# Sliding-window attention between two FFNs: turning the probabilities with VectorE's 32x32 transposes and copies inside SBUF instead of on TensorE

## The chip, the cores and the metric

The kernel runs on one core of one Trainium2 chip. The metric is the device time of one execution in microseconds (us), the median of several runs. The engines are PE (TensorE, matrix products), DVE (VectorE), ACT (ScalarE), POOL (GpSimd) and SP (SyncE, which only issues DMAs here). Everything is computed in fp32.

## The reference

Four sequences of 256 tokens, 512 wide, go through an FFN, an attention and the same FFN again, each on the layer-normalized input and added to it (the FFNs by half). The FFN is a 512x512 linear layer plus a mixture of 8 low-rank experts (rank 16, the best 2 of 8 by a router). The attention has 32 query heads, 8 key-value heads, a head dimension of 128, rotary embedding, and a causal window of 128 keys:

```python
q = _rope((x @ wq).reshape(B, S, 32, 128), pos)
k = _rope((x @ wk).reshape(B, S, 8, 128), pos)
v = (x @ wv).reshape(B, S, 8, 128)
scores = einsum('bqhgd,bshd->bhgqs', q.reshape(B, S, 8, 4, 128), k) * 128 ** -0.5
allowed = (j <= i) & (j > i - 128)
attn = softmax(where(allowed, scores, finfo.min))
out = einsum('bhgqs,bshd->bqhgd', attn, v).reshape(B, S, 4096) @ wo
```

## The kernel before, in words

The 1024 tokens are cut in two halves of two sequences. The first FFN runs over both halves, then the attention, then the second FFN. The attention is made of 32 **units** (h, g, b): half h, group g (a key-value head with its four query heads), sequence b of the half (lists at L842 and L843, main loop L960 to L1076). While a unit's softmax runs on the other engines, TensorE computes projections for later groups and output products of the unit before. All the projections use seven half-size products in place of eight, so sums of weights, of tokens and of results are formed on DVE and POOL.

A unit has 256 queries x 4 heads. They are taken in 8 blocks of 32 queries (4 with the first 128 tokens, 4 with the second), so that a block's 4 heads x 32 queries fill the 128 partitions. The steps of one unit:

- `scores` (L684): four products `sa` with the first 128 keys; DVE adds the mask and takes the row's maximum in one operation (L696) that writes into `probs`. Four products `sb` for the second 128 queries, each with the 128 keys of its window and a few more; DVE puts the right keys in place (L714) and takes maxima (L716).
- `exponentials` (L720): two small DVE operations make the negated, scaled maxima `nm` (L722, L723), then ACT takes 8 exponentials into `probs` with the row sums as a by-product.
- `normalize` (L734): a reciprocal on DVE and two multiplications of 128x512 on POOL (L738), in place on `probs`.
- `transposes` (L742): TensorE turns the 8 blocks (L746), so that keys lie on the partitions; ACT copies the first four out of PSUM (L750). Of the second four, the key rows belong partly to the first and partly to the second 128 tokens: DVE multiplies them by the 0/1 tiles `old` and `new` (L755) into two tiles.
- `values` (L761): `oa`, one product of 128x512 with the values for the first 128 queries, and `ob`, two of them for the second (L768); ACT copies both to `oT` (L771). `outputs` (L777) multiplies `oT` with the output weights (`y`, L794), in four steps that are put on the queue `late` and run inside the next unit.

The order of the instructions on PE, DVE, POOL and ACT is the order of the code (`manual_schedule`, L874 to L880; PE's and DVE's until three units are left). There is one buffer `probs`, so the next unit's `scores` follow this unit's `transposes` in the order. What runs around them depends on the unit:

- b = 0: the next group's `queries` (L517, steps "1" to "7"), mixed with the rest by a string (L979), in which "n" is `normalize`, "t" `transposes`, "y" an output product and "a", "w", "v", "k", "c", "d", "e" are FFN steps and sums: `"1yn6a27cy5d4yte3yw"`. Step "7" ends with DVE's `v` add (L512), "5" begins with the next add. The query results are rotated on DVE with the tables `cos_sb` and `sin_sb` (L484, L486) and summed on POOL (L492).
- b = 1: the next group's `keys` (L580, on odd n) or `project_values` (L624, on even n), in parts `both`, `second`, `others` (L995 to L1021), followed by sums of weights, a load of wk or wv on SP and output products.
- the last three units have no projections left; second-FFN steps fill them.

`transposes` are called by the string for b = 0 and otherwise at L1040 and L1041, just before the next unit's `scores`. The order of the loads on SP is found by a scheduler.

Of the kernel before, what the change touches and what calls it, by code (L numbers as in the profile page):

```python
# [29 lines left out]
BLK = 32  # L30
NB = P // BLK
EPS = 1e-5
SCALING = 32.0 / 16.0
SM_SCALE = HD ** -0.5
# [4 lines left out]
def macaron_kernel(  # L39
# [45 lines left out]
    cos_sb = const.tile([HD, S], F32, name="cos_sb")  # L85
    nc.sync.dma_start(out=cos_sb, in_=cos[:, :S])
    sin_sb = const.tile([HD, S], F32, name="sin_sb")
    nc.sync.dma_start(out=sin_sb, in_=sin[:, :S])

    weights = {}  # L90

# [118 lines left out]
        return bass.AP(tensor=w.tensor, offset=w.offset, ap=[w.ap[0], [-BLK, 2], w.ap[2]])  # L210


    probs = const.tile([P, 2 * NB, P], F32, name="probs")
    for e in range(NB - 1):
        nc.gpsimd.memset(probs[:, e, (e + 1) * BLK :], 0.0)


    old = const.tile([P, NB, BLK], F32, name="old")
# [462 lines left out]
        nc.scalar.copy(vS[h, g][:, i, :], pv[:, : 2 * HD])  # L681


    def scores(h, g, b):  # L684
        o = b * S
        q, k = qT[h, g][:, b], kT[h, g]
        pr = probs
        mx = sb.tile([P, 2 * NB], F32, tag="mx", bufs=3, name=f"mx_{h}_{g}_{b}")
        sm = sb.tile([P, 2 * NB], F32, tag="sm", bufs=3, name=f"sm_{h}_{g}_{b}")
        pa = score_bank(f"sa_{h}_{g}_{b}").rearrange("p (c k) -> p c k", k=P)  # L690
        for e in range(NB):
            n = (e + 1) * BLK
            nc.tensor.matmul(pa[:, e, :n], q[:, e], k[:, o : o + n], start=True, stop=True)  # L693
        for e in range(NB):
            n = (e + 1) * BLK
            nc.vector.tensor_tensor_reduce(  # L696
                pr[:, e, :n], pa[:, e, :n], mask[:, P - n :], SM_SCALE, -3.4e38,
                ALU.add, ALU.max, mx[:, e : e + 1],
            )
        pairs = []  # L700
        for p in range(NB // 2):
            pb = score_bank(f"sb_{h}_{g}_{b}_{p}")
            for r in range(2):

                m = 2 * p + r
                at = r * P + m * BLK
                nc.tensor.matmul(  # L707
                    pb[:, at : at + P + BLK], q[:, NB + m],
                    k[:, o + m * BLK : o + m * BLK + P + BLK], start=True, stop=True,
                )  # L710
# [5 lines left out]
            nc.vector.tensor_reduce(mx[:, NB + 2 * p : NB + 2 * p + 2], pb, AX.X, ALU.max)  # L716
            pairs.append(pb)
        return pr, mx, sm, pairs, f"{h}_{g}_{b}"

    def exponentials(pr, mx, sm, pairs, name):  # L720
        nm = sb.tile([P, 2 * NB], F32, tag="nm", bufs=3, name=f"nm_{name}")
        nc.vector.tensor_scalar(nm[:, :NB], mx[:, :NB], -1.0, None, ALU.mult)  # L722
        nc.vector.tensor_scalar(nm[:, NB:], mx[:, NB:], -SM_SCALE, None, ALU.mult)  # L723
        for n in range(2 * NB):
            keys_of = min(n + 1, NB) * BLK
            src, scale = (
                (pr[:, n, :], 1.0) if n < NB else (pairs[(n - NB) // 2][:, n % 2, :], SM_SCALE)
            )
            nc.scalar.activation(  # L729
                pr[:, n, :keys_of], src[:, :keys_of], AF.Exp, bias=nm[:, n : n + 1], scale=scale,  # L730
                accum_out=sm[:, n : n + 1],
            )

    def normalize(pr, sm):  # L734
        nc.vector.reciprocal(sm, sm)  # L735
        for n in range(0, 2 * NB, NB):
            w = pr[:, n : n + NB, :]
            nc.gpsimd.tensor_tensor(  # L738
                w, w, sm[:, n : n + NB].unsqueeze(2).to_broadcast([P, NB, P]), ALU.mult
            )  # L740

    def transposes(h, g, b, pr):  # L742
        def turn(n0, name):
            pt = ps.tile([P, NB, G, BLK], F32, tag="s", bufs=4, name=f"{name}_{h}_{g}_{b}")
            for e in range(NB):
                nc.tensor.transpose(pt[:, e, :, :], pr[:, n0 + e, :], ident)  # L746
            return pt

        p0 = sb.tile([P, NB, G, BLK], F32, tag="p0", bufs=1, name=f"p0_{h}_{g}_{b}")
        nc.scalar.copy(p0, turn(0, "t0"))  # L750
        pt = turn(NB, "t1")
        parts = []
        for n, w in enumerate((old, new)):
            part = sb.tile([P, NB, G, BLK], F32, tag=f"p1{n}", bufs=1, name=f"p1{n}_{h}_{g}_{b}")
            nc.vector.tensor_tensor(  # L755
                part, pt, w.unsqueeze(2).to_broadcast([P, NB, G, BLK]), ALU.mult
            )
            parts.append(part)
        return p0, parts

    def values(h, g, b, p0, p1):  # L761
        oT = sb.tile([HD, G, S], F32, tag="oT", bufs=4, name=f"oT_{h}_{g}_{b}")
        v = vS[h, g - g % 2]
        cols = ts(g % 2, HD)
        for i, parts in enumerate(([p0], p1)):
            po = mm_bank(f"o{'ab'[i]}_{h}_{g}_{b}")
            for n, part in enumerate(parts):
                nc.tensor.matmul(  # L768
                    po, v[:, 2 * b + n, cols], part, start=(n == 0), stop=(n == len(parts) - 1)
                )  # L770
            nc.scalar.copy(  # L771
                oT[:, :, ts(i, P)].rearrange("p j (e q) -> p e j q", e=NB),
                po.rearrange("p (e j q) -> p e j q", e=NB, j=G),
            )
        return oT

    def outputs(h, g, b, oT):  # L777
# [162 lines left out]
    def run(queue, n):  # L940
        for _ in range(min(n, len(queue))):
            queue.popleft()()
# [17 lines left out]
    for u, (h, g, b) in enumerate(units):  # L960
# [8 lines left out]
            nc.scalar.activation(root, eps, AF.Sqrt)  # L969
        parts = []  # L970

        def turn(at=(h, g, b), pr=ahead[0]):
            parts.extend(transposes(*at, pr))

        if b == 0 and n < len(groups):

            order = {0: "1n6kv2754t3", 4: "1yn6a27cy5d4yte3yw"}[len(late)]  # L979
            steps = queries(*groups[n], nc.vector.tensor_copy, ends)  # L980
            steps |= {
                "y": lambda: run(late, 1), "n": lambda: normalize(ahead[0], ahead[2]),
                "w": lambda: sum_o_weights(h, g), "v": lambda: project_v(0, 0, 2),
                "k": lambda: sum_weights("k", *groups[2]), "a": lambda: fill(left, 1),
                "t": turn, "c": None, "d": None, "e": None,
            }

            if g == NKV - 2 and h + 1 < NHALF:
                more_tokens = sum_tokens(h + 1, *(nc.gpsimd, nc.vector) * 2)
                steps |= {"c": more_tokens[3], "d": more_tokens[1], "e": more_tokens[2]}  # L990
            for step in order:
                if steps[step]:
                    steps[step]()
            ends.pop()()
        elif b == 1 and n + 1 < len(groups):  # L995
            both, second, others = begun
            both()
            run(late, 1)
            if g == NKV - 2 and h + 1 < NHALF:
                more_tokens[4]()  # L1000
            second()
            normalize(ahead[0], ahead[2])
            if n == 2:
                for t in behind:
                    measure(t, "a")
            if n % 2 == 1 and (h, g) != groups[NKV]:
                sum_weights("v", *groups[n + 1])
            others()
            fill(left, 4)
            turned = [behind.popleft() for _ in range(2 if behind and n in (4, 6) else 0)]  # L1010
            for t in turned:
# [8 lines left out]
            for t in turned:  # L1020
# [116 lines left out]
```

## Time and profile before

| | |
|---|---|
| runs, us | 766.15, 765.78, 765.36; median 765.78 |
| span of the profiled execution, us | 764.3 |
| PE busy, us | 757.1 (99%) |
| DVE, POOL, ACT busy, us | 560.1, 541.6, 210.3 (73%, 71%, 28%) |
| moved by DMA | 48.97 MB, mean 64 GB/s |
| transposes on PE (L746), one unit, on the chain | 0.87 us |
| ACT copy of turned blocks (L750) | 32 of 586 ns |
| value products (L768), one unit, on the chain | 0.86 us (oa), 1.72 us (ob) |

The span is the time from the first to the last instruction in the one execution that was profiled; the runs are timed from outside and take some 1.5 us more. A line of the groups or of a timeline names the engine, the line of the code, the operation and the tiles (output<-input), with partitions x elements; in a timeline the first two columns are start and duration in us, and a bracket at the end tells how long the engine had been idle and what released it. The chain is followed back from the last instruction, at each step to whatever it waited for.

### The profile page before, as it was taken

Reading aid. Unit: us, or ns where it says so; the run is one execution under the profiler, and the core shown is the slowest. Engines: PE = TensorE matmul, PEld = TensorE weight load, DVE = VectorE, ACT = ScalarE, POOL = GpSimd, SP = SyncE. Lnnn points to the kernel's source line nnn. Section 1 sums busy time; section 2 is a strip of 40 time slices with the busy share of each in tenths; the row PEclk is TensorE's granted clock in tenths of the full one; section 3 lists DMA queues with packets and bytes.
Section 4 is the critical chain, followed back from the end, with each engine's and each line's share of the span. In section 5 each row is a group of like instructions: output and inputs, shape, how many; then the busy total and the mean of one; then the engine's idle time right before and its main releaser. Section 6 shows DMA issues by size and latency. Waiting matters only on the chain.

```text
span 764.3 us, 11179 instructions
## 1 busy us (share of the span) xinstructions
PE 757.1 (99%) x3894; PEld 633.6 (83%) x3894; DVE 560.1 (73%) x1344; ACT 210.3 (28%) x749; POOL 541.6 (71%) x591
## 2 busy tenths in 40 slices
PE   8999999999999999999999999999999999999998
PEld 6877888888888888888888888888888888888866
DVE  5797885858675867668667867486867867595977
ACT  5421132422223130322222233213042222223331
POOL 6877775848767595769585788759575959865843
PEclk9999999999999999999999999999999999999999
DMA  9302111304030303112030303030301111010001
GB/s 318 123 1 83 52 59 30 109 1 138 1 111 28 111 28 97 42 57 83 20 118 1 129 9 111 28 111 29 107 31 56 56 49 63 1 56 28 2 27 56
DMA packets 29480, 48.97 MB, mean 64 GB/s; under 512 B 1136, under 2 KB 10352, under 8 KB 29424
## 3 DMA queue, kind: packets, MB, share of 16 engines
q1 hardware_dynamic: 29424, 48.26, 18.7%
q8 instruction: 31, 0.51, 0.3%
q14 instruction: 25, 0.20, 0.1%
HBM read 46.15 MB, written 2.10 MB: 63 GB/s over the span
## 4 chain that ended last, share of the span: by engine, by line
PE 96%; DVE 1%; DMA 1%; POOL 0%; SPq 0%; issue 0%; ACT 0%; DVEq 0%; ACTq 0%
PE q L533 25%; PE y L794 25%; PE ob L768 7%; PE k L590 6%; PE v L642 6%; PE sb L707 5%; PE sa L693 4%; PE oa L768 4%; PE t L746 4%; PE p_f L380 3%; PE po_f L380 2%; PE pa_f L344 2%; PE po_f L443 1%; DMA wb_sb<-in_w_base_dram 1%; PE po_f L360 1%; PE y L836 1%
## 5 line engine op out<-in xcount | busy, mean ns | idle before, releaser
L492 POOL TENSOR_TENSOR qT<-ra_q,rb_q 128x512 f32<-128x512 f32 x64 | 81.3, 1272 | 108.6 <-DVE rb_q L486 108.6
L486 DVE TENSOR_TENSOR rb_q<-q,sin_sb 64x512 f32<-64x512 f32 x128 | 88.0, 688 | 1.7
L750 ACT COPY p<-t 128x512 f32<-128x512 f32 x32 | 18.7, 586 | 211.7 <-PE t L746 211.7
L738 POOL TENSOR_TENSOR probs<-probs,sm 128x512 f32<-128x512 f32 x64 | 65.2, 1039 | 15.4 <-DVE sm L735 14.9
L794 PE MATMUL y<-wos,oT 128*128 128x256 f32 x248 | 63.7, 379 | 0.0
L794 PE MATMUL y<-wo,oT 128*128 128x256 f32 x248 | 63.7, 379 | 0.0
L794 PE MATMUL y<-wo,oTs 128*128 128x256 f32 x244 | 62.6, 379 | 0.0
L533 PE MATMUL q<-xs,wq 128*128 128x256 f32 x256 | 60.6, 379 | 0.2 <-DVE rb_k L486 0.2
L533 PE MATMUL q<-xa,wq 128*128 128x256 f32 x256 | 60.6, 379 | 0.0
L533 PE MATMUL q<-xs,wqs 128*128 128x256 f32 x256 | 60.5, 379 | 0.0
L768 PE MATMUL ob<-p,v 128*128 128x512 f32 x128 | 60.2, 592 | 0.0
L484 DVE TENSOR_TENSOR ra_q<-q,cos_sb 128x512 f32<-128x512 f32 x64 | 44.3, 691 | 20.4 <-PE q L533 14.8
L533 PEld LDWEIGHTS q<-xa,wq 128*128 128x128 f32 x256 | 48.4, 190 | 12.4 <-issue 6.2
L771 ACT COPY oT<-oa 128x512 f32<-128x512 f32 x32 | 18.7, 585 | 135.8 <-PE oa L768 135.8
L533 PEld LDWEIGHTS q<-xs,wq 128*128 128x128 f32 x256 | 48.6, 190 | 7.1 <-issue 0.5
L533 PEld LDWEIGHTS q<-xs,wqs 128*128 128x128 f32 x256 | 48.7, 190 | 6.6
L794 PEld LDWEIGHTS y<-wo,oT 128*128 128x128 f32 x248 | 46.6, 190 | 6.0
L794 PEld LDWEIGHTS y<-wo,oTs 128*128 128x128 f32 x244 | 46.4, 190 | 6.3
L794 PEld LDWEIGHTS y<-wos,oT 128*128 128x128 f32 x248 | 45.8, 190 | 5.3
L768 PEld LDWEIGHTS ob<-p,v 128*128 128x128 f32 x128 | 24.3, 190 | 30.6 <-issue 22.7
L729 ACT ACTIVATE probs<-probs,nm 128x32 f32<-128x32 f32 (+3 forms) x128 | 44.6, 351 | 11.4 <-DVE nm L722 6.0
L729 ACT ACTIVATE probs<-sb,nm 128x128 f32<-128x128 f32 x128 | 44.3, 353 | 0.0
(221 smaller groups left out, 1779.5 us busy)
## 6 DMA issues: line engine op xcount, KB each, us to landing
wq<-in_wq_dram SPq DMA_DIRECT2D x16, 1024.0 KB, 5.5
wo<-in_wo_dram SPq DMA_DIRECT2D x16, 1024.0 KB, 5.1
wk<-in_wk_dram SPq DMA_DIRECT2D x8, 512.0 KB, 3.4
wv<-in_wv_dram SPq DMA_DIRECT2D x8, 512.0 KB, 3.5
x<-in_x_dram SPq DMA_DIRECT2D x8, 256.0 KB, 6.1
out_dram<-x SPq DMA_DIRECT2D x7, 256.0 KB, 2.0
wb_sb<-in_w_base_dram SPq DMA_DIRECT2D x1, 1024.0 KB, 7.5
ar_sb<-in_w_ar_dram SPq DMA_DIRECT2D x1, 272.0 KB, 3.9
```

Source lines behind the costliest of these rows:

```text
L380: nc.tensor.matmul(bank[:, ts(i, D // 2)], lhs[j][m - 1][:, c, :], weights["bs"][m - 1][:, c, :], start=(m in (1, 5, 2, 4) and c == 0), st ...
L484: nc.vector.tensor_tensor(twice(a), twice(src), angle(cos_sb), ALU.mult)
L486: nc.vector.tensor_tensor(twice(b[o : o + half, :]), twice(src[i : i + half, :]), angle(sin_sb[o : o + half, :]), ALU.mult,)
L492: nc.gpsimd.tensor_tensor(dst, view(a), view(b), ALU.add)
L533: nc.tensor.matmul(bank[:, ts(j, S)], w[:, c, ts(j, HD)], x[:, c, :], start=(new and j == 0 and c == 0), stop=(c == 1), skip_group_check=True,
L590: nc.tensor.matmul(dst, w[n - 1][:, c, :], x[n - 1][:, c, :], start=(start and c == 0), stop=(c == 1), skip_group_check=True,)
L642: nc.tensor.matmul(bank[:, i, :], x[n - 1][:, c, ts(i, P)], w[n - 1][:, c, :], start=(start and i == 0 and c == 0), stop=(c == 1), skip_gr ...
L707: nc.tensor.matmul(pb[:, at : at + P + BLK], q[:, NB + m], k[:, o + m * BLK : o + m * BLK + P + BLK], start=True, stop=True,)
L729: nc.scalar.activation(pr[:, n, :keys_of], src[:, :keys_of], AF.Exp, bias=nm[:, n : n + 1], scale=scale, accum_out=sm[:, n : n + 1],)
L738: nc.gpsimd.tensor_tensor(w, w, sm[:, n : n + NB].unsqueeze(2).to_broadcast([P, NB, P]), ALU.mult)
L768: nc.tensor.matmul(po, v[:, 2 * b + n, cols], part, start=(n == 0), stop=(n == len(parts) - 1))
L794: nc.tensor.matmul(py[:, ts(i, D // 2)], lhs[n - 1][:, c, :], weights["os", h, g][n - 1][:, c, :], start=(i == 0 and c == 0), stop=(c == 1 ...
```

## The change

The score scale 128^-0.5 goes into the rotary tables: POOL multiplies `cos_sb` and `sin_sb` by its root once, right after their loads. DVE's mask operation now multiplies by -1 and takes a minimum, and the other reduction is negated, so `mx` holds negated maxima and serves as the bias of the exponentials; `nm` is gone.

`probs` is stored by blocks of 32 keys. A new constant tile `turned` takes the turned probabilities: DVE transposes all 32x32 squares of `probs` in place, with two operations, and 16 DMAs move the squares to their partitions, on SP's and ACT's queues in turn. DVE's `split` then makes the two tiles for `ob`, by a multiplication with `new` and a subtraction; `oa` reads `turned` directly. `turn_blocks` stands after step "2" in the strings of b = 0 ("T"), after `others` for b = 1, and at once after `normalize` in the last units; `split` stands where `transposes` stood. `normalize` works on pairs of key blocks, in two operations of the same size as before.

```diff
+    root_scale = SM_SCALE ** 0.5
+    for table in (cos_sb, sin_sb):
+        nc.gpsimd.tensor_scalar(table, table, root_scale, None, ALU.mult)
...
-    probs = const.tile([P, 2 * NB, P], F32, name="probs")
+    probs = const.tile([P, NB, 2 * NB, BLK], F32, name="probs")
+    turned = const.tile([P, G, 2 * NB, BLK], F32, name="turned")
     for e in range(NB - 1):
-        nc.gpsimd.memset(probs[:, e, (e + 1) * BLK :], 0.0)
+        nc.gpsimd.memset(probs[:, e + 1 :, e, :], 0.0)
+    for c in range(1, NB):
+        nc.gpsimd.memset(turned[ts(c, BLK), :, :c, :], 0.0)
...
-                pr[:, e, :n], pa[:, e, :n], mask[:, P - n :], SM_SCALE, -3.4e38,
-                ALU.add, ALU.max, mx[:, e : e + 1],
+                pr[:, : e + 1, e, :], blocks(pa[:, e, :n]), blocks(mask[:, P - n :]), -1.0, 3.4e38,
+                ALU.add, ALU.min, mx[:, e : e + 1],
...
-        nm = sb.tile([P, 2 * NB], F32, tag="nm", bufs=3, name=f"nm_{name}")
-        nc.vector.tensor_scalar(nm[:, :NB], mx[:, :NB], -1.0, None, ALU.mult)
-        nc.vector.tensor_scalar(nm[:, NB:], mx[:, NB:], -SM_SCALE, None, ALU.mult)
...
+    def turn_blocks(pr):
+
+        for c in range(0, NB, 2):
+            w = pr[:, c : c + 2].rearrange("p c n k -> p (c n k)")
+            nc.vector.transpose(w, w)
+        for c in range(NB):
+            for j in range(G):
+                (nc.sync if j % 2 == 0 else nc.scalar).dma_start(
+                    out=turned[ts(c, BLK), j, c:, :], in_=pr[ts(j, BLK), c, c:, :]
+                )
+
+    def split(h, g, b):
+        both = turned[:, :, NB:, :]
+        part = sb.tile([P, G, NB, BLK], F32, tag="part", bufs=1, name=f"part_{h}_{g}_{b}")
+        nc.vector.tensor_tensor(part, both, new.unsqueeze(1).to_broadcast([P, G, NB, BLK]), ALU.mult)
+        nc.vector.tensor_tensor(both, both, part, ALU.subtract)
+        return [turned[:, :, :NB, :]], [both, part]
...
-            order = {0: "1n6kv2754t3", 4: "1yn6a27cy5d4yte3yw"}[len(late)]
+            order = {0: "1n6kv2T754t3", 4: "1yn6a2T7cy5d4yte3yw"}[len(late)]
...
             others()
+            turn()
             fill(left, 4)
...
         else:
+            turn()
             run(late, len(late))
...
         if not parts:
-            turn()
+            part()
```

More of the change, by code (lines that the diff above doesn't have):

```diff
@@ L681, in project_v, with blocks @@
         nc.scalar.copy(vS[h, g][:, i, :], pv[:, : 2 * HD])
+    def blocks(t):
+        return t.rearrange("p (c k) -> p c k", k=BLK)
     def scores(h, g, b):
@@ L715, in scores @@
             pb = pb[:, :2, :]
-            nc.vector.tensor_reduce(mx[:, NB + 2 * p : NB + 2 * p + 2], pb, AX.X, ALU.max)
+            nc.vector.tensor_reduce(mx[:, NB + 2 * p : NB + 2 * p + 2], pb, AX.X, ALU.max, negate=True)
             pairs.append(pb)
@@ L720, in exponentials @@
     def exponentials(pr, mx, sm, pairs, name):
[L721 to L723 removed]
         for n in range(2 * NB):
[L725 removed]
+            dst = pr[:, : min(n + 1, NB), n, :]
             src, scale = (
[L727 removed]
+                (dst, -1.0) if n < NB else (blocks(pairs[(n - NB) // 2][:, n % 2, :]), 1.0)
             )
             nc.scalar.activation(
[L730 to L731 removed]
+                dst, src, AF.Exp, bias=mx[:, n : n + 1], scale=scale, accum_out=sm[:, n : n + 1]
             )
@@ L735, in normalize @@
         nc.vector.reciprocal(sm, sm)
-        for n in range(0, 2 * NB, NB):
-            w = pr[:, n : n + NB, :]
+        for c in range(0, NB, 2):
+            w = pr[:, c : c + 2]
             nc.gpsimd.tensor_tensor(
-                w, w, sm[:, n : n + NB].unsqueeze(2).to_broadcast([P, NB, P]), ALU.mult
+                w, w, sm.unsqueeze(1).unsqueeze(3).to_broadcast([P, 2, 2 * NB, BLK]), ALU.mult
             )
[L742 to L759, printed above, removed]
+    def turn_blocks(pr):
+        for c in range(0, NB, 2):
+            w = pr[:, c : c + 2].rearrange("p c n k -> p (c n k)")
[11 more added lines that the diff above has]
+        return [turned[:, :, :NB, :]], [both, part]
     def values(h, g, b, p0, p1):
@@ L764, in values @@
         cols = ts(g % 2, HD)
-        for i, parts in enumerate(([p0], p1)):
+        for i, parts in enumerate((p0, p1)):
             po = mm_bank(f"o{'ab'[i]}_{h}_{g}_{b}")
@@ L770, in values @@
                 )
[L771 to L774, printed above, removed]
+            nc.scalar.copy(oT[:, :, ts(i, P)], po.rearrange("p (j q) -> p j q", j=G))
         return oT
@@ L970, in macaron_kernel, with turn, part @@
         parts = []
-        def turn(at=(h, g, b), pr=ahead[0]):
-            parts.extend(transposes(*at, pr))
+        def turn(pr=ahead[0]):
+            turn_blocks(pr)
+        def part(at=(h, g, b)):
+            parts.extend(split(*at))
         if b == 0 and n < len(groups):
-            order = {0: "1n6kv2754t3", 4: "1yn6a27cy5d4yte3yw"}[len(late)]
+            order = {0: "1n6kv2T754t3", 4: "1yn6a2T7cy5d4yte3yw"}[len(late)]
             steps = queries(*groups[n], nc.vector.tensor_copy, ends)
@@ L984, in macaron_kernel @@
                 "k": lambda: sum_weights("k", *groups[2]), "a": lambda: fill(left, 1),
-                "t": turn, "c": None, "d": None, "e": None,
+                "T": turn, "t": part, "c": None, "d": None, "e": None,
             }
@@ L1008, in macaron_kernel @@
             others()
+            turn()
             fill(left, 4)
-            turned = [behind.popleft() for _ in range(2 if behind and n in (4, 6) else 0)]
-            for t in turned:
+            shifted = [behind.popleft() for _ in range(2 if behind and n in (4, 6) else 0)]
+            for t in shifted:
                 scale(t, "a")
@@ L1019, in macaron_kernel @@
             run(late, len(late) - 1)
-            for t in turned:
+            for t in shifted:
                 norm_attn(t, scaled=True)
         else:
+            turn()
             run(late, len(late))
```

## The prediction

> **What bounds the kernel now.** I read the page's head first, then the chain that ended last, then the timelines of one unit of each kind, and last the DMA rows.
>
> ```profile
> PE 757.1 (99%) x3894; PEld 633.6 (83%) x3894; DVE 560.1 (73%) x1344; ACT 210.3 (28%) x749; POOL 541.6 (71%) x591
> ...
> PEclk9999999999999999999999999999999999999999
> ...
> PE 96%; DVE 1%; DMA 1%; POOL 0%; SPq 0%; issue 0%; ACT 0%; DVEq 0%; ACTq 0%
> ...
> wk<-in_wk_dram SPq DMA_DIRECT2D x8, 512.0 KB, 3.4
> ...
> out_dram<-x SPq DMA_DIRECT2D x7, 256.0 KB, 2.0
> ```
>
> PE is busy for 99% of the span and makes 96% of the chain, at full clock in all forty slices. So whatever leaves PE's stream comes off the span, unless PE then waits; and a wait of PE adds to the span in full. The last two rows are used below for what a transfer costs. Now the chain through one unit, where b is 1 and the next group's keys are projected (columns: start, us, what):
>
> ```profile
> 272.37 3.45 PE y L794 x16
> 275.82 0.87 PE t L746 x8
> 276.69 0.89 PE sa L693 x8
> 277.59 1.09 PE sb L707 x8
> 278.68 1.73 PE y L794 x8
> 280.40 0.86 PE oa L768 x2
> 281.26 1.72 PE ob L768 x4
> ```
>
> PE goes from the transposes to the next unit's scores (sa, sb), two output products (y) and then the value products oa and ob, without a gap.
>
> **What is saved.** The 8 transposes cost 0.87 us of the chain. 32 units make 32 x 0.87 = **27.8 us**. The 32 ACT copies (L750, 586 ns each) and the 64 small DVE operations for the negated maxima go as well, but those engines are busy for 28% and 73% and hardly in the chain: nothing from them.
>
> **What is added: a longer way from probabilities to oa.** It is now: DVE transposes both halves of `probs` (call this T), SP and ACT issue 16 copies, all 16 land, and only then may oa and DVE's split start. The built order of instructions shows three things that the diff does not. The DMAs share eight semaphores in turn, so a unit's ninth to sixteenth each wait for one of the first eight to land: two waves, four per queue in each. The split and oa wait for all sixteen, but oa does not wait for the split; ob does. And while the split waits on DVE, what stands behind it there waits too: the next unit's mask-and-maximum (L706 of the new code), then the next adds. These feed PE only behind oa.
>
> Call A the time from T's release to the last landing:
> - the first transpose. No row shows one. DVE's operations of 128x512 take 0.67 to 0.70, those of 128x256 take 0.42, two of 64x512 1.39. I take 0.69, the same shape, with ends 0.42 and 1.39. The second runs beside the first wave.
> - a landing, twice in a row. No row shows a copy inside SBUF or one of 32 KB. Stores of 256 KB land 2.0 us after issue, the last two stores of 128 KB after 1.90 and 1.84. The line through 1.84 and 2.0 gives 1.72 at 32 KB. Loads of 512 and 1024 KB take 3.4 and 5.5, a line that begins at 1.3. The slowest row with an empty queue is the first x load, 2.47. I take 1.75, the stores being nearest, with ends 1.3 and 2.47.
> - three issues before the wave's last. Issue rows on SP take 0.33 (the store at 760.66) to 0.53 (cos, at 7.06), most of them 0.37. I take 0.40.
> - three hand-overs between engines and queues, 0.1 each, an estimate from gaps such as that from `rb_q`'s end at 333.32 to POOL's start at 333.39.
>
> A = 0.69 + 1.75 + 3 x 0.40 + 1.75 + 3 x 0.1 = **5.7 us**; the lower ends of landing and issue give 4.6, the upper ones 7.5.
>
> One place where a rule of the Trainium skill speaks against the change: "DMA: Bandwidth & Descriptors", sections "Anatomy of one DMA" and "Rules for kernel authors", puts about 2.0 us of fixed cost on each DMA of GpSimd's path, and advises against many small ones. The nearest rows here (1.84 for 128 KB) say a little less. An estimate by that page: 2.0 plus 0.08 for 32 KB makes A 6.4, and the time 782 instead of the forecast.
>
> The split is two dependent operations between SBUF tiles, 2 x 0.7 plus a hand-over, 1.5 us. oa (0.86) hides the first part; where oa is already late, ob costs PE **0.6** more.
>
> **Where A fits, kind by kind.** I took the end of the DVE instruction behind which T stands (or the end of normalization on POOL, if later), and the start of oa, both before; oa may then come 0.87 earlier.
>
> Seven units of the kind above (b=1, keys):
>
> ```profile
> 275.45 1.39 DVE L486 TENSOR_TENSOR rb_k<-k,sin_sb 64x512 f32<-64x512 f32 x2
> 276.87 0.69 DVE L804 TENSOR_TENSOR z<-y,z 128x512 f32<-128x512 f32 x1
> 277.47 0.68 DVE L811 TENSOR_TENSOR x<-y,x 128x512 f32<-128x512 f32 x1
> 278.07 0.68 DVE L755 TENSOR_TENSOR p<-t,old 128x512 f32<-128x512 f32 x1
> 278.67 0.68 DVE L755 TENSOR_TENSOR p<-t,new 128x512 f32<-128x512 f32 x1
> ```
>
> T is queued behind `rb_k`, which ends at 276.84. oa starts 3.41 us later by PE's timeline, 2.54 without the transposes. PE waits 5.7 - 2.54 = 3.16, and 0.6 for the split: 3.76 x 7 = **26.3**. Here DVE was the engine with no slack: T can't come earlier in its queue.
>
> Units with b=0 (queries; fifteen):
>
> ```profile
> 331.93 1.39 DVE L486 TENSOR_TENSOR rb_q<-q,sin_sb 64x512 f32<-64x512 f32 x2
> 333.35 0.69 DVE L512 TENSOR_TENSOR v_q<-q,u_q 128x512 f32<-128x512 f32 x1
> 334.68 0.69 DVE L804 TENSOR_TENSOR z<-y,z 128x512 f32<-128x512 f32 x1 [0.64 <-PE y L794]
> ...
> 342.79 0.68 DVE L755 TENSOR_TENSOR p<-t,old 128x512 f32<-128x512 f32 x1
> ```
>
> T stands behind the second `rb_q` (end 333.32), and the landing, 5.7 later, comes at 339.0, before the split's place at 342.8. T pushes `v_q` back by 1.3, but DVE idles 0.64 and then 1.03 before the next two adds: 0. Without that cover it is up to 1.3 in each. One is different (the unit that also makes the second half's token sums): normalization ends late on POOL, at 462.42, 0.4 after the add behind T could start. T takes 1.3 more: **1.8** with the hand-over, 4.6 if PE isn't already late there.
>
> The other b=1 units (values): oa starts 7.88 after the last v add in two, 7.01 in four, 5.78 in one. Less 0.87: 7.01, 6.14, 4.91. With the split's 0.6: 0 for two, 5.7 + 0.6 - 6.14 = 0.16 for each of four (0.7), **1.4** for one. A wv load is issued on SP just ahead of these copies; if its 512 KB hold them up, by at most its own 3.4, more is lost there.
>
> The last three units: T follows normalization. 5.88 and 7.38 to oa give 1.3 and 0; in the last, PE has 1.7 us of FFN products ahead of oa in the new order: 5.7 + 0.6 - 4.2 = **2.1**.
>
> Sum: 26.3 + 1.8 + 0.7 + 1.4 + 1.3 + 2.1 = 33.6 lost against 27.8 saved: **+5.8**. The two table scalings on POOL come ahead of the first FFN's token sums, 1.0 to 1.9 us of POOL against 2.5 us of slack to PE there: 0, or up to 1.9 if that slack is gone. The eight issues on ACT (8 x 0.4 = 3.2 per unit, less the 0.59 copy) lie in its 72% of idle time. The profiled span is 764.3, the median of the runs 765.78, so 1.5 lies around the span: 764.3 + 5.8 + 1.5 = 771.6, about **772**.
>
> One us of A is worth 10 below 5.5 (seven keys units, three single ones), 15 above (the four value units and the late b=0 unit join), 17 from 6.4. Even with the median: A = 5.2. A difference within 0.2% (1.5 us) can't be told from none: A from 5.05 to 5.35.
>
> **Rivals.**
> 1. *Forecast (0.50):* A between 5.35 and 6.6. The wait for two landings in the seven keys units eats the whole saving: 767 to 785, likeliest 772. For it: oa's 2.54 us there hold one landing, never two.
> 2. *Landings are slow, or PE slows after waiting (0.16):* A from 6.6 to 7.5, 785 to 801. For it: 16 copies meet in the same DMA engines; against: the DMA row of the page is mostly at 0 to 3 tenths. The granted clock was full throughout, but no PE wait of 3 us stands in this trace, so it can't show what such a wait does. The page "TensorE: Matmul & The Clock Gate", section "HAM oscillation", says that idling over about 3.4 us halves the clock for a while; it lies just at the size expected here.
> 3. *Faster (0.24):* one mechanism, landings inside SBUF that are quicker than any store. At 1.3 us A is 4.8, and with issues of 0.33 it is 4.6: the keys units lose 2.7 each, 18.6 in all, and the rest 3 to 4; the time is 760. It decides at A = 5.05, a landing of 1.4.
> 4. *Same (0.10):* A from 5.05 to 5.35, 764.3 to 767.3.
>
> That the change doesn't do what it says is excluded by the built order: no transposes on PE, 512 copies.
>
> **Range and chances.** Slower is cases 1 and 2, 0.66; same 0.10; faster 0.24. The range, 760 to 790, leaves out the end of case 2 and the quickest part of case 3. The forecast's own: 767 to 785.
>
> **What would show it.** Right: in the seven keys units PE idles 3 to 4 us before oa, put down to DMAs from `probs` to `turned`; copies land in 1.6 to 1.9 us, the ninth issued just after the first landed; none of it in b=0 units; PE's busy time 28 us less. Wrong: all sixteen issued at once; landings near 1.3 or above 2.3; a granted clock under 0.99; PE waiting for q adds in b=0 units, which would mean that T has no cover there.

## The result and the profile after

The changed kernel takes 849.34 us, the median of 4 runs (848.22 to 850.11), against 765.75 before: a ratio of 1.109, with a 95% interval of 1.107 to 1.110. Slower was forecast, but 6 us of it and not 84, and the time lies 59 us above the end of the range. So most of what follows looks for a loss that my sum doesn't contain.

The page after, head, clock, chain and the rows of the copies:

```profile
PE 769.8 (91%) x3638; PEld 613.8 (73%) x3638; DVE 607.1 (72%) x1344; ACT 190.8 (23%) x717; POOL 555.4 (66%) x596
...
PEclk9999989999899989998999979998999899999989
...
PE 41%; DVE 26%; POOL 9%; ACTq 8%; DMA 5%; issue 5%; SPq 3%; ACT 1%; DVEq 0%; POOLq 0%
...
turned<-probs SPq DMA_DIRECT2D x64, 32.0 KB, 2.1
turned<-probs ACTq DMA_DIRECT2D x64, 32.0 KB, 2.0
turned<-probs SPq DMA_DIRECT2D x64, 28.0 KB, 1.8
```

PE went from 99% busy to 91%, and from 96% of the chain to 41%. DVE and POOL stand in the chain with 26% and 9%, ACT's DMA queue with 8%. And there are 8s and 7s in the clock's row, where before there were only 9s: the mean granted clock is 0.962. The copies themselves land some 1.8 to 2.1 us after their issue, close to the 1.75 that I had taken.

One of the seven keys units in the timeline after:

```profile
206.72 1.30 DVE L752 STREAM_TRANSPOSE probs<-probs 128x512 f32<-128x512 f32 x2
207.45 4.95 SPq L755 DMA_DIRECT2D turned<-probs  x8
214.34 0.69 DVE L762 TENSOR_TENSOR part<-turned,new 128x512 f32<-128x512 f32 x1 [5.14 <-DMA turned<-probs]
214.40 2.04 PE L773 MATMUL oa<-turned,v 128*128 128x512 f32 x2 [5.03 <-DMA turned<-probs]
215.06 0.69 DVE L763 TENSOR_TENSOR turned<-turned,part 128x512 f32<-128x512 f32 x1
```

The wait stands exactly where it was forecast: T directly behind `rb_k`, then PE idle before oa until `turned` has landed. But it is 5.03 us and not 3.2. And oa then takes 2.04 us, where its row in the timeline before shows 1.02. The stretches of 2 us around it tell why (columns: window, length, busy time of PE, PEld, DVE, ACT, POOL with counts, granted clock, DMA share, GB/s):

```profile
208.00:210.00 2.00, 1.38 (x7) 0.87 (x5) 1.19 (x3) 0.00 (x0) 1.92 (x3) 1.00 0.30 74
210.00:212.00 2.00, 0.00 (x0) 0.00 (x0) 0.00 (x0) 0.00 (x0) 1.92 (x3) 0.91 0.34 86
212.00:214.00 2.00, 0.00 (x0) 0.00 (x0) 0.00 (x0) 0.00 (x0) 1.23 (x2) 0.50 0.21 54
214.00:216.00 2.00, 1.60 (x2) 0.63 (x3) 1.63 (x7) 0.00 (x0) 0.00 (x0) 0.50 0.00 0
216.00:218.00 2.00, 2.00 (x4) 0.88 (x4) 1.93 (x10) 0.58 (x1) 0.00 (x0) 0.50 0.00 0
218.00:220.00 2.00, 2.00 (x8) 1.31 (x7) 0.45 (x1) 0.74 (x3) 0.07 (x1) 0.89 0.00 0
```

Here the clock was granted at half some 2.3 us after PE fell idle, and it stayed there until about 4.1 us after PE had begun to work again. In the seven keys units the first time goes from 2.3 to 4.6 us and the second from 4.1 to 8.4; the last section tells why they scatter. Over the whole trace, PE's busy time weighted with the missing clock (a microsecond at half clock counts half) makes 25 us.

By kind of unit, from one oa to the next, the change of the time against before:

| units | forecast, net of 0.87 saved in each | measured |
|---|---|---|
| seven b=1, keys | +20.2 | +36.9 |
| seven b=0 right behind them | -4.3 | +19.5 |
| seven b=1, values | -4.0 | +10.2 |
| other six b=0 | -5.2 | -1.1 |
| first unit and last four | -1.0 | +16.8 |

The first row was half foreseen. That the units behind the keys units lose, which should have won, was not.

### The profile page after: what moved, and what is told of

Same layout as the page of the kernel before. It is cut to its first block, busy times and chain, and to the rows that moved or that the text cites. A ratio compares the mean times of both kernels' runs of the same rounds, so it can differ in the third digit from the quotient of the medians.

```text
span 846.5 us, 11853 instructions
## 1 busy us (share of the span) xinstructions
PE 769.8 (91%) x3638; PEld 613.8 (73%) x3638; DVE 607.1 (72%) x1344; ACT 190.8 (23%) x717; POOL 555.4 (66%) x596
## 4 chain that ended last, share of the span: by engine, by line
PE 41%; DVE 26%; POOL 9%; ACTq 8%; DMA 5%; issue 5%; SPq 3%; ACT 1%; DVEq 0%; POOLq 0%
PE q L540 15%; ACTq L755 8%; PE ob L773 6%; PE y L796 5%; DMA turned<-probs 4%; DVE rb_q L493 4%; PE v L649 3%; SPq L755 3%; DVE turned L763 2%; PE k L597 2%; PE oa L773 2%; DVE part L762 2%; DVE probs L752 2%; DVE q L519 2%; POOL wos L130 2%
## 5 line engine op out<-in xcount | busy, mean ns | idle before, releaser
L125 POOL TENSOR_TENSOR oTs<-oT 128x256 f32<-128x256 f32 x31 | 22.5, 726 | 90.9 <-ACT oT L776 90.9
L773 PE MATMUL oa<-turned,v 128*128 128x512 f32 x64 | 41.4, 733 | 43.4 <-DMA turned<-probs 43.1
L762 DVE TENSOR_TENSOR part<-turned,new 128x512 f32<-128x512 f32 x32 | 32.7, 1021 | 59.1 <-DMA turned<-probs 59.0
L540 PE MATMUL q<-xa,wq 128*128 128x256 f32 x256 | 62.6, 389 | 0.0
L540 PEld LDWEIGHTS q<-xa,wq 128*128 128x128 f32 x256 | 51.0, 200 | 15.7 <-issue 8.7
L773 PEld LDWEIGHTS oa<-turned,v 128*128 128x128 f32 x64 | 12.0, 221 | 49.7 <-issue 48.5
L130 POOL TENSOR_TENSOR wos<-wo 128x512 f32<-128x512 f32 x31 | 45.1, 1455 | 4.3 <-PE y L796 3.1
```

The source lines that it names most:

```text
L125: nc.gpsimd.tensor_tensor(dst, p, q, op)
L130: engine.tensor_tensor(dst, p, q, ALU.subtract)
L540: nc.tensor.matmul(bank[:, ts(j, S)], w[:, c, ts(j, HD)], x[:, c, :], start=(new and j == 0 and c == 0), stop=(c == 1), skip_group_check=True,
L762: nc.vector.tensor_tensor(part, both, new.unsqueeze(1).to_broadcast([P, G, NB, BLK]), ALU.mult)
L773: nc.tensor.matmul(po, v[:, 2 * b + n, cols], part, start=(n == 0), stop=(n == len(parts) - 1))
```

## The experiments

Each time is a median; the kernel before took 765.9 to 766.1 beside them. Mixed kernels are those that turn some units in the new way and some in the old.

**Leave the copies out** (e1).

```diff
-        for c in range(1, NB):
-            nc.gpsimd.memset(turned[ts(c, BLK), :, :c, :], 0.0)
+        nc.gpsimd.memset(turned, 0.01)
...
-        for c in range(NB):
-            for j in range(G):
-                (nc.sync if j % 2 == 0 else nc.scalar).dma_start(
-                    out=turned[ts(c, BLK), j, c:, :], in_=pr[ts(j, BLK), c, c:, :]
-                )
```

> The 16 copies are left out: oa and the split read a tile that is filled once with a constant, so the attention's values are not computed from the probabilities; the two DVE transposes, the split and everything else stay. Theory 1 (the copies' way from issue to landing, what PE's idling does to its clock, and ACT's queue being filled with issues make the whole loss): without them PE never waits for the turned tile, and the time is 736.5 (span before less the transposes' 27.8) plus 1.5 around it plus a few us for late units: 738 to 752. Theory 2 (the loss is on DVE: it is busy for 607 us instead of 560, its two new operations between SBUF tiles take 1.02 us instead of 0.69): the time stays over 800.

Measured: **777.5 us** (1.015 of before, 1.013 to 1.016). Neither theory. The copies make 71.9 us of the loss, but without any of them the kernel is still slower than before, although the transposes have left PE. The timeline of this kernel in the same place as above:

```profile
197.60 0.77 DVE L756 TENSOR_TENSOR part<-turned,new 128x512 f32<-128x512 f32 x1
197.70 1.02 PE L767 MATMUL oa<-turned,v 128*128 128x512 f32 x2
197.90 1.59 POOL L125 TENSOR_TENSOR wqs<-wqs,wq 128x512 f32<-128x512 f32 x1
198.40 1.64 DVE L757 TENSOR_TENSOR turned<-turned,part 128x512 f32<-128x512 f32 x1
...
200.19 1.10 PE L767 MATMUL ob<-turned,v 128*128 128x512 f32 x2 [1.47 <-DVE mx L705]
```

oa starts at once now, but ob waits 1.47 us for the split's end (the releaser's name is that of DVE's next instruction). The split's second operation takes 1.64 us while POOL adds weights (which itself takes 1.59 instead of 1.28); in the changed kernel's unit shown above (215.06), with POOL idle, it takes 0.69. The mean of the second operation over all units is 1.52 here, and 1.12 in the changed kernel, where the waiting for copies often leaves POOL with nothing to do. The Trainium skill, page "SBUF — State Buffer", section "SBUF: two separate sides", states that a DVE operation with two SBUF inputs and a GpSimd operation that reads SBUF exclude each other for a whole instruction; both numbers agree with it. The old multiplications read PSUM and took 0.68 each.

**Which of DVE's two new parts.** On top of e1, e5 also drops the split and e6 the transposes instead:

```diff
# e5
-        nc.vector.tensor_tensor(part, both, new.unsqueeze(1).to_broadcast([P, G, NB, BLK]), ALU.mult)
-        nc.vector.tensor_tensor(both, both, part, ALU.subtract)
-        return [turned[:, :, :NB, :]], [both, part]
+        return [turned[:, :, :NB, :]], [both, both]
# e6
-            nc.vector.transpose(w, w)
```

> The 16 copies and also DVE's split are left out: oa and both products of ob read one tile filled with a constant; the two DVE transposes stay. Without copies the time was 777.5, some 40 more than the 738 that the missing transposes alone would give. Theory S (the split makes most of the 40: its second operation takes 1.52 us on average where I had 0.7, and ob waits 1.3 to 2.6 us for it in ten units): 744 to 753, what is left being the late normalization in unit 18 (8 us). Theory T (the two transposes, 1.3 us in DVE's order in front of adds that PE waits for, make most of it): 763 to 775.

> The 16 copies and the two DVE transposes are left out, the split stays; the attention's values are not computed from the probabilities. Theory S (the split makes most of the 40 us): 765 to 775, as without copies, less the 8 us of unit 18, where v_q stood behind the transposes. Theory T: 742 to 752. If both push the same thing (the transposes put the split 1.2 us later on DVE, the split makes ob wait), this run and the one before both win 20 or more, and their gains together exceed the 40.

Measured: **750.9** without the split, theory S; **758.4** without the transposes, in neither theory's window. The two gains, 26.5 and 19.1, together exceed the 37.6 that there are to win, nearly as the third case has it. And with all three left out (e10), to close the sum:

> Copies, DVE transposes and split are all left out (oa and ob read a tile of constants). Closing the sum: if the loss is made of these three alone, the time is 764.3 - 27.8 + 1.5 = 738, from 736 to 741; if the new layout of the probabilities or the shifted normalization costs something of its own, more than 743.

Measured: **739.9**. So the saving is real: 765.8 - 739.9 = 25.9 us. From there the split alone costs 18.5, the transposes alone 11.0, both together 37.6 and not 29.5, since the transposes put the split later (in the keys units ob waits 1.3 to 1.5 us for it in e1 and at most 0.25 in e6). Unit by unit e5 wins 0.87 or 0.88 in 27 of the 32: T as work for DVE is covered, as I had said. Its loss is in a few places, above all in the late b=0 unit, where PE waits 4.9 us: DVE stands at T, which waits for normalization on POOL, in front of `v_q`. In e6, on the other hand, 12 of the 16 b=1 units win only 0.05 to 0.16.

**What the copies' time is made of.** All on one queue (e2), or only half of them (e7):

```diff
# e2
-                (nc.sync if j % 2 == 0 else nc.scalar).dma_start(
+                nc.sync.dma_start(
# e7
-            for j in range(G):
-                (nc.sync if j % 2 == 0 else nc.scalar).dma_start(
+            for j in range(0, G, 2):
+                (nc.sync if j == 0 else nc.scalar).dma_start(
```

> All 16 copies on SP's queue, none on ACT's. With both queues at once an issue takes 0.62 us on each. Theory A (an issue takes that long on its queue, whatever the other does): 16 issues take 16 x 0.62 = 9.9 us instead of 4.9, the last landing is 5 us later, and in the some 17 units where PE waits now the time grows by 5 each: 920 to 940. Theory B (both queues share what makes the descriptors, 0.31 us per copy in all): the landing stays where it is, and the waits that ACT's filled queue makes (2.25 us in unit 2, 2.09 in unit 18, some more at the values' copies) go: 838 to 849.

Measured: **983.3**. Theory A, and more than it said. On one queue alone, an issue follows the other after 0.63 us, as on each of the two queues together, so it is the queue's own time and the second queue halves the total. The 16 on one queue took 9.4 us from the first issue to the last. The time grew by 134 and not by 71 to 91: PE now waits in b=0 units as well (it is idle for 101 us more), and the mean clock falls to 0.906 (33 us more by the records).

> Only 8 of the 16 copies, 4 per queue (heads 1 and 3 are left at a constant, so their values are wrong); all else as in the changed kernel. The last landing comes 4 x 0.62 = 2.5 us earlier, 4.8 us after the transposes' release in place of 7.3. Theory 1 (PE waits for the landing beyond its 2.5 us of room, then loses its clock, and ACT's queue is blocked for half as long): 7 x 2.3 of waiting in the keys units, nothing in the values units, hardly any clock loss: 785 to 800, more than half of the 72 us between no copies (777.5) and all (849.3) gone. Theory 2 (each copy costs the same wherever it ends, by its load on queues and SBUF): halfway, 808 to 818.

Measured: **818.2**. The waits in the keys units shrank as theory 1 said, to 2.2 to 2.5 us; but the gain of 31 us is less than half of 72, and the time lies just past the end of theory 2's window. PE's timeline shows what I had wrong:

```profile
206.69 1.92 PE L772 MATMUL oa<-turned,v 128*128 128x512 f32 x2 [2.49 <-DMA turned<-probs]
209.19 2.05 PE L772 MATMUL ob<-turned,v 128*128 128x512 f32 x2 [0.59 <-DVE mx L705]
```

oa takes 1.92 here too: a wait of 2.5 us was enough to halve the clock, in each of the seven keys units, and now nearly all of the slow stretch falls on work. The clock's loss by the records is 22 us, against 25 with all copies.

**What the slow clock costs.** Needless products stand ahead of oa in its bank, in the seven keys units (eleven in e3, five in e8):

```diff
+            if i == 0 and b == 1 and g % 2 == 0 and (h, g) != groups[-2]:
+                for _ in range(11):
+                    nc.tensor.matmul(po, ident, wb_sb[:, 0, :], start=True, stop=True)
```

> In the seven keys units 11 needless products of 128x512 (0.43 us each, 4.7 us) stand ahead of oa in oa's own bank, so that PE works while it waits for the copies; oa starts no earlier. Theory 1 (after some 2.5 us of idling the granted clock falls to a half, and it comes back only some 4 us after work has begun again): the clock stays full around these units, and 1.5 to 2.6 us are won in each, 10 to 18 us in all: 831 to 839. Theory 2 (the low clock in the records costs nothing, because what follows oa waits for DVE's split in any case): within 3 us of 849.

Measured: **862.0**. This run is a miss of mine and tells neither: a 128x512 product is two records in fp32, so the fillers took 9.6 us per unit and pushed oa back. With five:

> As the run with eleven fillers, but five: a 128x512 product in fp32 shows as two records and took 0.87 us, not 0.43, so eleven were 9.5 us and pushed oa back by 3.9. Five are 4.35 us inside the 5.0 us of waiting; oa starts no later. Theory 1 (the halved clock after the wait costs 1.5 to 2 us in each of the seven keys units): 835 to 840. Theory 2 (it costs nothing): 848 to 851.

Measured: **840.2**, 9.1 us less, just past the end of theory 1's window. With useless work ahead of oa the kernel is faster; the mean clock rises from 0.962 to 0.983. Up to oa the keys units lose as much as before (36.3 us against 36.9), and the seven units behind them lose 7.8 in place of 19.5; some of it is given back in the values units (13.9 against 10.2), in three of which the clock now falls as it did not before. So the clock is a cause and not only a symptom, worth nearly 12 us in these places and 9 in all.

**Start earlier** (e4).

```diff
             normalize(ahead[0], ahead[2])
+            if n % 2 == 1:
+                turn()
...
             others()
-            turn()
+            if n % 2 == 0:
+                turn()
```

> In the seven keys units the DVE transposes and the copies stand directly behind normalize, ahead of the last keys' additions and rotations, some 4.2 us earlier on DVE. Theory 1 (oa waits only for the landing): the wait of 5.0 us shrinks to about 1, the clock stays full there, and 7 x (4 + 1.5 to 2.6) = 38 to 46 us are won: 803 to 811. Theory 2 (the work that the transposes push back on DVE is late next: the key banks come free 1.3 us later and PE waits for them, and the split is the limit): less than half of it, over 828.

Measured: **830.4**, 19 us won: theory 2's window, by a little. oa's wait of 5.0 us shrinks to 2.8 or less, but ob's wait for the split comes back in its place (1.3 to 1.9 us), and in four of the seven units the clock still falls. In five of them issuing SP's eight copies takes 6.4 to 7.5 us and not 4.4 to 4.7. The timeline of SP's queue shows a weight load just ahead of them:

```profile
199.79 0.37 SPq L99 DMA_DIRECT2D wk<-in_wk_dram  x1
200.70 6.94 SPq L755 DMA_DIRECT2D turned<-probs  x8
```

The third copy on SP was issued at 203.97, 2.7 us behind the second. It waits for a semaphore that it shares with the first copy on ACT's queue, and that one had landed only at 203.95, 3.25 us after its issue and not 1.8. The five copies issued up to 202.2, on both queues, took 2.4 to 3.3 us, and all landed after the load had (203.56). So copies issued 0.9 us behind a load of 512 KB came late here, and by the shared semaphores so did issues behind them.

**The first part of the change alone** (e9: the kernel before, with scale in the tables and the negated minimum as bias, without `nm`):

> The kernel before with only the first part of the change: score scale in the rope tables, negated minimum as bias, no nm operations; the transposes stay on TensorE. Theory 1 (the whole difference is made by the new way of turning): the same as before within 1.5 us, or up to 2 us less. Theory 2 (the changed mask operation, the reductions or the tables cost something): over 768.

Measured: **767.0**, 0.9 us slower (1.0002 to 1.0020). It is no part of the loss worth speaking of, and no gain either.

**A mixed kernel.** The b=0 units had room, so I kept the new way only in 11 of them, and let TensorE turn the rest. One buffer serves both layouts.

```diff
+    def on_dve(h, g, b):
+        n = h * NKV + g
+        return b == 0 and (2 <= n <= 8 or 10 <= n <= 13)
...
-        def part(at=(h, g, b)):
-            parts.extend(split(*at))
+        def part(at=(h, g, b), wide=wide):
+            parts.extend(split(*at) if wide else transposes(*at))
```

> TensorE turns the probabilities as before, except in 11 units with b=0 (groups 2 to 8 and 10 to 13), where the changed way is kept: there 12.6 us lie between the transposes' place and oa, no value of ACT's queue is urgent, and normalization is in time. ACT clears a few squares where one buffer serves both layouts. Theory 1 (the new way costs nothing where it is covered, and PE's 0.87 us are won): 11 x 0.6 to 0.87 = 7 to 10 us less than before, 756 to 759. Theory 2 (the DVE transposes and the slower split push on PE in these units too): 764 to 768.

Measured: **767.2** (1.0005 to 1.0022). Each of the 11 units wins 0.88, and the unit behind it gives 0.65 to 0.75 back (2.84 in one). This is the clearest view of the split's price, with no wait for a copy in the way. The timeline of the end of such a unit:

```profile
176.56 1.25 DVE L814 TENSOR_TENSOR part<-turned,new 128x512 f32<-128x512 f32 x1
...
177.23 1.72 POOL L130 TENSOR_TENSOR wos<-wo 128x512 f32<-128x512 f32 x1
...
177.85 1.64 DVE L815 TENSOR_TENSOR turned<-turned,part 128x512 f32<-128x512 f32 x1
...
180.91 1.39 DVE L502 TENSOR_TENSOR rb_q<-q,sin_sb 64x512 f32<-64x512 f32 x2
...
182.35 0.73 PEld L606 LDWEIGHTS k<-xs,wks 128*128 128x128 f32 x4 [0.30 <-DVE rb_q L502]
182.35 1.13 PE L606 MATMUL k<-xs,wks 128*128 128x256 f32 x4
...
183.37 0.73 PEld L854 LDWEIGHTS y<-wos,oT 128*128 128x128 f32 x4 [0.29 <-POOL wos L130]
...
185.51 0.51 PEld L606 LDWEIGHTS k<-xs,wk 128*128 128x128 f32 x3 [0.55 <-DVE u_k L528]
```

The split ends before ob needs it. But behind it on DVE stands the rotation `rb_q`, which ends at 182.30, and PE's next product starts at 182.35, into the bank (the part of PSUM) that the rotation has read. PE seems busy, yet the unit is 0.74 longer. Product by product against the kernel without the split (e12, next), this first place accounts for 0.17 of it. Another 0.15 are lost at 183.37, where PE waits for sums of weights (`wos`) on POOL, which the split has slowed, and the largest part, 0.41, at 185.51, behind DVE's add `u_k`, further back in the order. Other units of this kind show the same three places.

Then three edits of the mixed kernel. Without its split (e12, the edit of e5):

> The mixed kernel (11 units turned by DVE and copies, the rest on TensorE), with DVE's split left out in those 11 units, so both products of ob there read the same undivided tile and the values are wrong. Theory S (the split leaves DVE behind, and PE pays for it in the next unit): the 0.65 to 0.75 us of the ten b=1 units and the 2 us of unit 13 are won: 767.2 - 9 = 756 to 759. Theory T (the two transposes or the copies do it): 763 to 768.

Measured: **757.7** (0.988 to 0.991 of before). Theory S: what was given back is won. Next, the split ahead of step 4's rotation (e13):

```diff
             add(bank, bank, state["u2"])
+            if hook:
+                hook()
             turn(0, 2, bank)
...
-            steps = queries(*groups[n], nc.vector.tensor_copy, ends)
+            steps = queries(*groups[n], nc.vector.tensor_copy, ends, hook=part if wide else None)
```

> The mixed kernel with the split in the 11 units ahead of the rotation of step 4, some 2 us earlier on DVE, where POOL computes nothing beside it; the copies have just landed there. Theory P (half of the split's cost is that POOL's operations on SBUF stand beside it): its operations take 0.69 us each in place of 1.25 and 1.64, 1.5 us of DVE are won, less up to 0.5 of waiting for the last copy, and the next unit's 0.65 to 0.75 us come back: 757 to 762. Theory B (any two more operations on DVE push PE as much, or DVE waits as long for the copies as it wins): 765 to 769.

Measured: **781.5**, a miss of both. The same kernel again, to read where the time goes:

> The kernel with the early split again, for a profile at full clock: span 779 to 780. Theory W (DVE waits in its order for the last copy, and the rotation behind it, whose reading frees the bank of TensorE's next product, comes late): DVE idles before the split for 0.5 to 1.5 us in each of the 11 units, and PE for about as long behind it. Theory P' (POOL's operation on SBUF still stands beside the split): no wait for copies, the split's operations over 1 us.

Measured: 782.1, and theory W in the main. In 10 of the 11 units both operations of the split take 0.69 now that POOL is idle beside them, so the cost of POOL's neighbourhood is shown from both sides; but DVE stands idle in front of them for 0.7 to 3.0 us in every one of the 11 units. PE pays for it by another way than theory W has it: only 3.9 us of its waits are for the rotation `rb_q`, and 11.4 us for POOL's sums of weights, which stand in POOL's order behind the sum of that late rotation. DVE's wait in one unit:

```profile
175.53 0.69 DVE L816 TENSOR_TENSOR part<-turned,new 128x512 f32<-128x512 f32 x1 [1.58 <-DMA turned<-probs]
176.25 0.69 DVE L817 TENSOR_TENSOR turned<-turned,part 128x512 f32<-128x512 f32 x1
```

Last, half the split: ob = whole x old values + new part x (new values - old values), in the mixed kernel (e14) and with all units on TensorE (e15).

```diff
         nc.vector.tensor_tensor(part, both, new.unsqueeze(1).to_broadcast([P, G, NB, BLK]), ALU.mult)
-        nc.vector.tensor_tensor(both, both, part, ALU.subtract)
...
+                nc.vector.tensor_tensor(v[:, 2 * i + 1], v[:, 2 * i + 1], v[:, 2 * i], ALU.subtract)
```

> The mixed kernel with half the split: ob = whole x old values + new part x (new values - old values), so only the multiplication by the mask stays per unit (one DVE operation; in the units turned on TensorE ACT copies the whole out of PSUM), and the differences of the values are made once for two groups, on DVE at the start of a unit with b=0. Theory S (PE pays for the time by which the split leaves DVE behind): the mixed kernel without any split took 757.7, with all of it 767.2; with one operation of 0.7 to 1.3 us instead of 2.9 it lies nearer the former: 757 to 762. Rival (the first operation's wait for POOL is the part that counts, or the new differences push as much): 764 to 768.

> The same with all 32 units turned on TensorE, as in the kernel before. PE is the bound there and keeps all its work, so the 20 us that DVE gets rid of win nothing: 765 to 768. If it is as fast as the mixed kernel, the mixed one owes its time to this and not to the transposes that left PE.

Measured: **758.5** for the mixed kernel (0.989 to 0.992 of before), **767.0** with TensorE turning all (1.0004 to 1.0022). So this version beats both, and by the transposes that left PE: in PE's timeline the product of above starts behind its predecessor without a wait,

```profile
181.59 1.03 PE L606 MATMUL k<-xa,wk 128*128 128x256 f32 x4
182.45 1.03 PE L606 MATMUL k<-xs,wks 128*128 128x256 f32 x4
```

and 10 of the 11 units keep their 0.88 (the other 0.75); one unit behind them still gives 1.35 back.

## Why the prediction was wrong, step by step

- **Saved, 27.8 us:** right; 25.9 with everything new left out (e10).
- **A = 5.7 us:** 7.23 (206.72 to 213.95). The transpose (0.67 to 0.72 each) and the landing (1.8) were right. What failed is the term "three issues before the wave's last, 0.40 each". From one issue of these copies to the next on a queue it takes 0.63 us, so when four are out the first has already landed, the two waves never come about, and the time is 0.73 to the first issue, 4.69 for seven more (most 0.63, one slower), and 1.81 for the last landing. My 0.40 came from rows of loads and stores of 128 to 1024 KB, most of them 0.37, which tell nothing of a small copy inside SBUF; and the first loads have longer rows than the 0.53 that I named as the largest, 0.55 at 4.21 and 0.68 at 5.76. With 7.23 my own sum gives 771.6 + 10.5 + 14 = 796: inside the range of the rival "landings are slow", though for another reason, and still 53 short.
- **The split, "0.6 more" where oa is late and nothing elsewhere:** the largest hole. I priced it as two operations of 0.7 and asked only when ob could start. It took 1.02 and 1.12 on average (1.07 and 1.52 without copies) instead of 2 x 0.68, and it stands in DVE's order ahead of adds and rotations that free PE's banks. Together with the transposes it costs 37.6 us without a single copy.
- **b=0 units, "0":** T's cover held, as e5 shows. The units lost because the split of the b=1 unit before them, and its slow clock, run into their time.
- **The other b=1 units (values), 2.1:** they lost 10.2 in the table, where -4.0 was forecast. In five of the seven, PE waited 8.3 us in all for the landing before oa, by the same longer A (7.2 to 8.2 there); in the other two it waited 3.4 us for a copy of ACT's.
- **The late b=0 unit, 1.8:** it lost 7.5 (6.6, and the 0.87 that it should have won), but hardly by this term. T's wait for POOL is the right mechanism, and where PE comes in time it costs what the alternative of 4.6 said (5.1 in e5). In the changed kernel PE was already 4.8 us late there, by the slow clock and ob's wait for the split, and `v_q` cost it only 0.3 more; a late copy of ACT's made 2.3.
- **ACT's issues "lie in its 72% of idle time":** an average where the stage counts. In two units PE needed a copy that ACT makes and that stood behind the issues:

```profile
140.90 0.58 ACT L801 COPY z<-y 128x512 f32<-128x512 f32 x1 [11.27 <-DMA turned<-probs]
```

  PE waited 2.25 us for it there and 2.09 in the other. Over the whole trace, PE's waits for operations of ACT make 15.7 us; there is none of them without the copies, and 1.1 us with all copies on SP's queue (e2). My sum had this term at nothing.
- **The clock:** named in the rival, left out of the sum. By the records it takes 25 us (some 23 more than without copies). Five fillers ahead of oa won 9 of it back. The Trainium skill's page "TensorE: Matmul & The Clock Gate", section "HAM oscillation", gives a gap of over 3.4 us as the limit; here a wait of 2.5 us was enough (e7).

In all: 765.8 - 25.9 (transposes off PE) + 11.0 (T on DVE) + 18.5 (split) + 8 (both together) + 71.9 (copies) = 849.3. Of the 71.9, PE's idle time is 44 (76.7 against 32.5 us outside its busy time) and the clock some 23; 2 more are there because the two profiled executions differ by 69.9 and not 71.9. What stays open: 3 us of PE's busy time, and why the issue of so small a copy takes 0.63 us.

## What to carry to other kernels

An engine at 73% is not free: ask of each new operation what stands behind it in its engine's order and which bank that frees, for the bill may come a unit later, on another engine, and look like busy time. A chain of small copies costs issue time times their number per queue, then one landing; count it from a row of the same kind, or measure it alone first. And move work off the bound engine only in the stages that have the room: the same way of turning lost 84 us everywhere and, in 11 chosen units with half the split, won 7.

## What the runs showed of the hardware

- A DVE operation on two SBUF tiles of 128x512 took 0.69 us alone and, in the mixed kernel, 1.25 and 1.64 beside a POOL operation on SBUF, which itself went from 1.27 to 1.60 and 1.72.
- Copies of 20 to 32 KB from SBUF to SBUF left SP's or ACT's queue one every 0.63 us, whatever their size and whatever the other queue did, and most landed 1.8 us after their issue (up to 3.3 where a load of 512 KB was on its way, in the unit of e4 shown).
- TensorE's granted clock changed in these traces only at the ends of steps of 3.41 us, and it followed PE's busy share of such a step, not the length of one wait. In the 17 traces of the two kernels and of every run but e13 it fell from full to a half after each of the 63 steps in which PE was busy for less than 44%, after 6 of 16 between 44% and 51%, and after none of some 3700 above that. It came back after each of the 69 steps with PE busy for 85% or more, and after none of 52 under 83%. (The ends of PE's work are modelled in these records, so the shares hold to a few per cent.) So where a wait falls counts: the wait of 2.49 us in e7 lay in one step and left it 27% busy, and the clock fell; one of 2.68 us in the changed kernel, ahead of oa at 168.50, fell on two steps, left them 58% and 54% busy, and it did not.
